# A four-layer image kernel: order of the first loads, the point at which C is spread, and values made beside keys

## The chip, the cores and the metric

One core of a Trainium2 chip. The metric is device time in microseconds (us) of one execution. Three runs of the kernel before gave 5076.55, 5076.93 and 5080.12 us; the median is 5076.93. The engines are named as in the profile: PE is TensorE (matmuls), PEld its weight loads, DVE is VectorE, ACT is ScalarE, POOL is GpSimd, and SP is SyncE, which here does nothing but issue DMAs.

## The reference

The input is x of shape (2, 128, 64, 64), float32: two images of 128 channels. Four layers follow each other. Cut to what matters here:

```python
# layer 0: 1x1 embed, two blocks of (layernorm, mamba, residual, layernorm, ffn, residual), 1x1 out, + x
u, z = split(norm(t) @ in_w.T);  u = silu(causal_conv4(u))
dt, Bm, Cm = split(u @ xproj_w.T, [8, 24])        # 8 + 16 + 16 columns
dt = softplus(dt @ dt_w.T + dt_b)
h = exp(dt * A) * h + (dt * u) * Bm               # 256 x 16 states, over 4096 positions
y = (sum_n(h * Cm) + u * D) * silu(z);  t = y @ out_w.T + t
# layer 1: attention over all 4096 positions with 3x3 convolutions
q, k, v = conv3x3(x, Wq), conv3x3(x, Wk), conv3x3(x, Wv)
x = x + conv1x1(softmax(q.T @ k / sqrt(128)) @ v.T, Wo)
# layer 2: the same shape of attention with dense (1x1) q, k, v
# layer 3: 3x3 convolutions at four scales, attention over the four, layernorm, 1x1 fusion
```

## The kernel before

The program's order on every engine is the order in which it was written (a manual schedule); tiles come from pools with a fixed number of buffers, and an instruction that takes a used buffer waits for the last reader.

**Start.** SP issues, in this order: constants `kc`, vectors `vec`, the eight chunks of image 0 (L93, 512 positions each), the embedding weights `we` (L125), and for each of the two mamba blocks `wl`, `cw` (taps, spread over the partitions, and the input projection) and `wd`; then three `raw` (the 3x3 weights of layer 1's q, k, v) and the chunks of image 1. For each block VectorE makes the folded taps `wu` (L152), and TensorE and VectorE spread the decay rates `an` to `am` (L155 to L162). `fold(which)` (L177 to L188, ten VectorE operations and two stores) turns one `raw` into the 18 filter slices of a reduced 3-tap convolution and stores them in DRAM as `ufold`.

**Layer 0.** There are 32 items (image, block, chunk of 512 positions), and each has 32 slots. In `slot(i, todo, t_)` one slot does one scan (L388, 128 lanes x 512 positions) of item i; four scans make a group, eight groups an item. A group's decay comes from `decay` (L377, ACT), its input from `times_b` (h = bb * pdu, L370), its result is multiplied with `cb` on POOL (L391) and summed on TensorE (`py`, L403). `spread_dt` (L359) copies a strip of dt to a tile `dtb` with four DMAs, `spread_dtu` (L364) does the like for dt*u on TensorE into `pdu`. Everything else is in `background(i)`, a list of what goes beside the scans in each slot, for items i-2 to i+2: input projection `pu`, `xproj` (`pd`, L321), `spread_bc` (L328 to L335), softplus, the norm (`pc`, `var`, `rs`, `pr`, `cen`, `xn`), gating, and the feed-forward (`ph`, `hid`, `pf`). Items -2 and -1 have no scans; in them the first items are prepared. `spread_bc` of item n is called once, in slot 14 of the item before:

```python
dr = dp.tile([2 * DS, CH], F32, name="dr", tag="dr")
nc.sync.dma_start(dr, st[i]["dbl"][R:])
for k in range(2):
    o = st[i]["bc", k] = sp.tile([P, 4, CH], F32, name=("bb", "cb")[k], ...)
    for q in range(4):
        nc.sync.dma_start(o[32 * q : 32 * q + 32]..., src.to_broadcast([32, 4 * CH]))
```

Both `bb` (B) and `cb` (C) go through DRAM (`dr`) and come back spread over 32 partitions.

**From layer 0 to layer 1.** While the last items end, `beginning()` is run step by step, as many steps in each slot as the string `beside` says. It loads q's and k's filters from `ufold` to the ring `uw`, and makes the queries of the first chunk and all keys of image 0. One conv over a chunk of 16 rows (1024 positions) is `inputs` (12 VectorE operations on `xt`, L599 to L610), `products_by` (18 matmuls `pa`, `pb`, L622) and `outputs` (2 ACT and 9 VectorE operations, L639 to L648). There are four chunks.

**Layers 1 and 2.** Four runs: (layer 1, image 0), (layer 1, image 1), (layer 2, image 0), (layer 2, image 1). A run has 128 units. In each unit TensorE makes 128 x 1024 scores (`pq`, L725), VectorE takes them out with the row maximum (L730), ACT takes exponentials every fourth unit (L740), `turn` (L755) transposes 128 x 2048 of them with one VectorE instruction in 32 x 32 blocks, and POOL, ACT's queue and SP's queue (L762 to L766) move the blocks to `pt`. LAG = 14 units later `product` (L775) multiplies `pt` with the turned values `vt`. The values of a layer-1 run are made in unit 13 by `values(r)`: per chunk `inputs` again, products with v's filters, `outputs` to `vs`, and `turned(cc)` (8 transposes `pvt` on TensorE and 2 copies on ACT). The two halves of v's filters are loaded in unit 1, and the first chunk's `inputs` are made in units 6 to 11.

Of the kernel before, what the change touches and what calls it, by code (L numbers as in the profile page):

```python
# [14 lines left out]
N = H * W  # L15
P = 128
# [51 lines left out]
def tile_conv_seq(ctx: ExitStack, tc, x, consts, vecs, wemb, wlay, wconv, wdt, wqkv, wsmall, wms, out):  # L68
# [23 lines left out]
    for c in range(NCH):  # L92
        nc.sync.dma_start(xv(0, c), x[0, :, c * RPC : (c + 1) * RPC, :])  # L93
# [20 lines left out]
    with tc.manual_schedule(), ExitStack() as s:  # L114
# [25 lines left out]
        wl, wu, wd, am = [], [], [], []  # L140
        for l in range(NL):
            w = wp.tile([P, NWL - DI], F32, name=f"wl{l}")
            nc.sync.dma_start(w, wlay[l][:, DI:])
            cw = sp.tile([P, KC + 1, DI], F32, name="cw", tag="h", bufs=5)
            nc.sync.dma_start(cw[:, :KC, :].rearrange("p k d -> p (k d)"), wconv[l : l + 1, :].to_broadcast([P, KC * DI]))
            nc.sync.dma_start(cw[:, KC, :], wlay[l][:, :DI])
            d = wp.tile([R, DI], F32, name=f"wd{l}")
            nc.sync.dma_start(d, wdt[l])

            u = wp.tile([P, KC, DI], F32, name=f"wu{l}")  # L150
            for k in range(KC):
                nc.vector.tensor_tensor(u[:, k, :], cw[:, KC, :], cw[:, k, :], ALU.mult)  # L152
            an = wp.tile([P, NJ * DS], F32, name=f"an{l}")
            nc.scalar.activation(an, vec[:, VEC[f"A_log{l}"] : VEC[f"A_log{l}"] + NJ * DS], AF.Exp)
            nc.vector.tensor_scalar(an, an, -1.0, None, ALU.mult)  # L155
            a = wp.tile([P, NJ, 4, 4], F32, name=f"am{l}")
            for g in range(4):
                pa = mm.tile([P, NJ, DS], F32, name="pa", tag="mm")
                nc.tensor.matmul(pa.rearrange("p j n -> p (j n)"), lhsT=four(g), rhs=an, start=True, stop=True)
# [3 lines left out]
            wl.append(w), wu.append(u), wd.append(d), am.append(a)  # L163
        raws = []
        for which in range(3):
            raw = sp.tile([P, 3, 3, C], F32, name="raw", tag="h", bufs=5)
            nc.sync.dma_start(raw.rearrange("p y x c -> p (y x) c"), wqkv[:, which])
            raws.append(raw)
        for c in range(NCH):
            nc.sync.dma_start(xv(1, c), x[1, :, c * RPC : (c + 1) * RPC, :])  # L170

        def fold(which):

# [150 lines left out]
            st[i]["dbl"] = sp.tile([NX, CH], F32, name="dbl", tag="dbl")  # L324
            nc.scalar.copy(st[i]["dbl"], st[i].pop("pd"))

        def spread_bc(i):

            dr = dp.tile([2 * DS, CH], F32, name="dr", tag="dr")
            nc.sync.dma_start(dr, st[i]["dbl"][R:])  # L330
            for k in range(2):
                o = st[i]["bc", k] = sp.tile([P, 4, CH], F32, name=("bb", "cb")[k], tag=("bb", "cb")[k], bufs=2)
                for q in range(4):
                    src = dr[k * DS + 4 * q : k * DS + 4 * q + 4, :].rearrange("(o m) f -> o (m f)", o=1)
                    nc.sync.dma_start(o[32 * q : 32 * q + 32].rearrange("p m f -> p (m f)"), src.to_broadcast([32, 4 * CH]))  # L335

        def dtproj(i, j):
            st[i]["pt", j] = mmt("pt")
# [131 lines left out]
        def background(i):  # L470

            todo = [[] for _ in range(NSL)]

            def at(t, f, *a):
                todo[t].append((f, a))

            n, p, q, r = i + 1, i - 1, i - 2, i + 2
            if has(q):
                at(3, gelu, q)
                at(6, ffn_down, q, (0, 1)), at(7, ffn_down, q, (2, 3)), at(9, ffn_add, q)  # L480
                at(11, out_mm, q), at(12, out_add, q)
            if has(p):
                at(7, y_out, p, 1), at(7, gate, p)
                at(9, mix_out, p), at(11, mix_add, p)
            if has(n):
                at(0, pu_taps, n, 0, (0, 1)), at(1, pu_taps, n, 0, (2, 3)), at(2, pu_out, n, 0)
                at(3, pu_taps, n, 1, (0, 1)), at(4, pu_taps, n, 1, (2, 3)), at(5, pu_out, n, 1)
                at(13, xproj, n), at(14, xproj_out, n), at(14, spread_bc, n)
                at(15, dtproj, n, 0), at(16, dtproj, n, 1), at(17, soft_plus, n), at(18, dt_end, n)
            if has(i):  # L490
                at(1, pz_mm, i, 0), at(3, pz_out, i, 0)
                at(5, pz_mm, i, 1), at(6, pz_out, i, 1)
            if has(i) or has(n):
                at(11, silu, i, n)
            if i == -1:
                for k in range(3):
                    at(8 * k + 2, fold, k)
            pair = [(k, second) for k, second in ((p, True), (r, False)) if has(k)]
            if has(r):
                at(10, embed, r), at(11, embed_out, r)  # L500
            w, m = {}, len(pair)
            for k, (it, second) in enumerate(pair):
                at(12 + 2 * k, ln_centre, w, k, it)
                at(13 + 2 * k, ln_square, w, k, it)
                at(27, ln_spread, w, k, m), at(28, ln_scale, w, k, it)
# [15 lines left out]
        def slot(i, todo, t_):  # L521
            t = i * NSL + t_
            g, m = divmod(t, 4)
            if m == 0 and 0 <= g + 3 < NG:
                spread_dt(g + 3)
            if m == 0 and 0 <= g + 1 < NG:
                spread_dtu(g + 1)
            if m == 0 and g % 2 == 1 and 0 <= g - 3 < NG:
                y_pair(g - 3)
# [1 line left out]
                scan(t)  # L531
            if 0 <= t + 4 < NT:
                decay(t + 4)
            if m == 3 and 0 <= g + 1 < NG:
                times_b(g + 1)
            for f, a in todo[t_]:
                f(*a)
# [72 lines left out]
                lambda: stt(d[5], x1(1), 4.0, d[5], ALU.mult, ALU.add),  # L610
            ]

        def products_by(which):

            pa = pss.tile([P, 4, QG], F32, name="pa", tag="s")
            pb = psq.tile([P, 2, QG], F32, name="pb", tag="q")
            for slot, dst in enumerate((pa[:, 2, :], pa[:, 0, :], pa[:, 3, :], pa[:, 1, :], pb[:, 0, :], pb[:, 1, :])):
                d = dlo[:, slot] if slot < 4 else sta["dhi"][:, slot - 4]
                for y in range(3):
                    rhs = d[:, y : y + 16, :].rearrange("p h j -> p (h j)")  # L620
                    lhsT = uw[:, where[which, slot // 3], 3 * (slot % 3) + y, :]
                    nc.tensor.matmul(dst, lhsT=lhsT, rhs=rhs, start=(y == 0), stop=(y == 2))  # L622
                yield
            return pa, pb
# [50 lines left out]
        def keys(r):  # L675
            k = sta["k"] = spa.tile([P, N], F32, name="k", tag="k")
            chunks(r, 1, lambda cc: k[:, cc * 4 * QG : (cc + 1) * 4 * QG])

        def values(r):
            vt = sta["vt"] = sp.tile([P, N // P, C], F32, name="vt", tag="vt")  # L680
            vs = {}

            def turned(cc):
                for i in range(2):
                    pt = psa.tile([P, 4, P], F32, name="pvt", tag="acc")
                    for a in range(4):
                        at = (4 * i + a) * P
                        nc.tensor.transpose(pt[:, a, :], vs[cc][:, at : at + P], ident)
                    at = (2 * cc + i) * 4
                    nc.scalar.copy(vt[:, at : at + 4, :], pt)  # L690

            def to(cc):
                if cc > 1:
# [124 lines left out]

        NALL = len(runs) * NU
        LO, HI = 0, 1  # L820
        def beginning():

            for which, half in ((0, LO), (0, HI), (1, LO)):
                load(which, half)
            for f in inputs(0, 0):
                f()
            yield
# [3 lines left out]
            outputs(*pp, [sta["q", 0, i] for i in range(4)], bias(0, 0))  # L831
            load(1, HI)
            k = sta["k"] = spa.tile([P, N], F32, name="k", tag="k")
            for cc in range(NCC):
# [12 lines left out]
        for k in range(8, 2 * NSL):  # L847
            if k == NSL:
                todo = background(NI + 1)
# [2 lines left out]
            slot(NI + k // NSL, todo, k % NSL)  # L852
        for _ in steps:
            pass
        layers.close()
        sp = s.enter_context(tc.tile_pool(name="ats", bufs=1, reuse_waits="tile"))
        psa = s.enter_context(tc.tile_pool(name="atpa", bufs=2, reuse_waits="tile", space=PSUM))
        psm = s.enter_context(tc.tile_pool(name="atpm", bufs=1, reuse_waits="tile", space=PSUM))
        for now in range(NALL + LAG + 10):
            r, u = divmod(now, NU)  # L860
            w = now % 8
            if now < NALL:
# [510 lines left out]
```

## Time and profile before

| what | value |
|---|---|
| median of 3 runs | 5076.93 us |
| profiled execution, its own time | 5077.7 us |
| its span, first to last instruction | 5075.9 us |
| mean granted TensorE clock | 0.948 |
| first scan starts / last scan ends | 84.94 / 2102.9 us |
| first `pq` of layer 1 | 2186.42 us |
| TensorE busy 2271 to 4400 | 2082.90 of 2129 us |
| layer 3 | about 4400 to the end |
| `cb<-dr`, `uw<-ufold`, `dtb<-dt`, from issue to landing | 7.6, 3.7, 2.0 us |

A timeline line gives the start, the duration, engine, line, operation, tiles and the number of instructions merged in it; the bracket has the engine's idle time before it and what released it. Lines of SP are the issuing of DMAs, not the transfers. In the page's section 2 each digit is the busy share of one of 40 slices (127 us each) in tenths.

### The profile page before, as it was taken

The page shows a single profiled execution, that of the slowest core. Times are in us where ns is not written, and L with a number is a line of the kernel's source. Part 1 is how long each engine was busy: PE and PEld are TensorE (multiplying, and loading weights), DVE is VectorE, ACT ScalarE, POOL GpSimd, SP SyncE. Part 2 cuts the span into 40 slices and gives each one's busy share as a digit, 9 for nine tenths or more (in the row PEclk, how much of TensorE's full clock was granted, in tenths as well). Part 3 has the DMA queues.
Part 4 walks back from the last instruction along what each step waited for, and adds up shares of the span by engine and source line. Part 5 has one row for each costly group of instructions (what it writes and reads, how often), then busy time and mean ns, then how long its engine had stood idle before and what let it go on. Part 6 is the DMA issues. An engine that isn't in the chain of part 4 may idle for free.

```text
span 5075.9 us, 48999 instructions
## 1 busy us (share of the span) xinstructions
PE 4683.8 (92%) x14797; PEld 2250.9 (44%) x14797; DVE 4097.5 (81%) x4416; ACT 2366.9 (47%) x3221; POOL 2316.3 (46%) x1948
## 2 busy tenths in 40 slices
PE   5889999999988899889999999999999999999997
PEld 1222222222222222356666666666666666333332
DVE  5999999999999999788888878667766775667775
ACT  4677777777777777522222222333333332323332
POOL 2777776766777777413332233233333332322331
PEclk8898889988999989899999999999999999999998
DMA  5333333333333333124443344444444443000000
GB/s 149 72 69 68 70 71 70 72 69 68 69 70 68 72 72 71 46 54 102 105 102 84 77 104 103 118 97 111 111 100 99 112 111 77 5 5 7 7 7 7
DMA packets 237016, 373.86 MB, mean 74 GB/s; under 512 B 88000, under 2 KB 88400, under 8 KB 228432
## 3 DMA queue, kind: packets, MB, share of 16 engines
q1 hardware_dynamic: 187600, 303.55, 25.8%
q10 hardware_dynamic: 49152, 67.17, 5.8%
q8 instruction: 118, 1.93, 0.2%
q14 instruction: 146, 1.20, 0.1%
HBM read 92.18 MB, written 9.83 MB: 20 GB/s over the span
## 4 chain that ended last, share of the span: by engine, by line
PE 47%; POOL 21%; DVE 13%; issue 11%; DMA 3%; ACT 3%; SPq 2%; ACTq 0%; DVEq 0%; POOLq 0%
POOL h L391 16%; PE po L775 13%; PE pq L725 13%; DVE tr L755 3%; DMA pt<-tr 2%; PE pf L1060 2%; SPq L766 2%; PE py L403 2%; PE pqkv L1087 2%; PE pu L292 1%; PE pw L1146 1%; POOL dtu L351 1%; PE pfus L1211 1%; POOL z L414 1%; PE psc L1111 1%
## 5 line engine op out<-in xcount | busy, mean ns | idle before, releaser
L762 POOL COPY pt<-tr 32x512 f32<-32x512 f32 x1024 | 656.1, 641 | 1468.2 <-DVE tr L755 738.8
L388 DVE TENSOR_TENSOR_SCAN h<-da,carry,h 128x512 f32<-128x512 f32 x1024 | 1241.4, 1266 | 60.4 <-ACT da L377 31.6
L391 POOL TENSOR_TENSOR h<-h,cb 128x2048 f32<-128x2048 f32 x256 | 1161.1, 4536 | 20.8 <-POOL carry L390 0.2
L725 PE MATMUL pq<-k,q 128*128 128x512 f32 x2048 | 965.1, 594 | 11.2 <-DVE sc L730 8.8
L775 PE MATMUL po<-pt,vt 128*128 128x256 f32 x4096 | 967.5, 380 | 2.4 <-DMA pt<-tr 2.4
L740 ACT ACTIVATE sc<-sc,nm 128x2048 f32<-128x2048 f32 x256 | 510.6, 1995 | 937.2 <-DVE nm L736 641.7
L730 DVE TENSOR_SCALAR_CACHE_REDUCE sc<-pq 128x1024 f32<-128x1024 f32 x512 | 624.9, 1222 | 359.8 <-PE pq L725 337.9
L775 PEld LDWEIGHTS po<-pt,vt 128*128 128x128 f32 x4096 | 780.5, 191 | 293.9 <-issue 211.1
L377 ACT ACTIVATE da<-dtb,am 128x512 f32<-128x512 f32 x1024 | 681.7, 684 | 222.1 <-DVE h L388 210.6
L755 DVE STREAM_TRANSPOSE tr<-sc 128x2048 f32<-128x2048 f32 x256 | 591.6, 2311 | 65.8 <-DMA pt<-tr 60.5
L370 DVE TENSOR_TENSOR h<-bb,pdu 128x2048 f32<-128x2048 f32 x256 | 581.7, 2272 | 77.4 <-PE py L403 29.3
L403 PE MATMUL py<-h,sel 128*32 128x512 f32 x2048 | 511.5, 643 | 1.6 <-POOL h L391 1.6
L725 PEld LDWEIGHTS pq<-k,q 128*128 128x128 f32 x2048 | 384.5, 191 | 289.5 <-issue 247.1
L364 PE MATMUL pdu<-dtu,fsel 128*128 128x512 f32 x512 | 326.5, 724 | 101.9 <-DVE h L370 101.8
L403 PEld LDWEIGHTS py<-h,sel 128*32 128x32 f32 x2048 | 115.7, 118 | 415.9 <-issue 408.9
L292 PE MATMUL pu<-xn,wu 128*128 128x512 f32 x512 | 246.2, 615 | 3.0 <-ACT xn L282 2.1
L364 PEld LDWEIGHTS pdu<-dtu,fsel 128*128 128x128 f32 x512 | 96.2, 215 | 308.3 <-DVE h L370 187.6
L390 POOL COPY carry<-h 128x4 f32<-128x4 f32 x256 | 47.5, 185 | 388.1 <-DVE h L388 383.5
L1153 DVE TENSOR_TENSOR ov<-v,pw 128x2048 f32<-128x2048 f32 x64 | 146.2, 2285 | 68.5 <-PE pw L1146 68.5
L1087 PE MATMUL pqkv<-f,ws 128*128 128x512 f32 x384 | 189.7, 619 | 3.0 <-DVE prod L1104 2.3
L1157 POOL TENSOR_TENSOR ov<-ov 128x2048 f32<-128x2048 f32 x16 | 72.6, 4537 | 257.6 <-DVE ov L1153 257.6
L351 POOL TENSOR_TENSOR dtu<-dt,u 128x1024 f32<-128x1024 f32 x32 | 75.0, 2345 | 189.7 <-ACT dt L345 189.7
(241 smaller groups left out, 5344.1 us busy)
## 6 DMA issues: line engine op xcount, KB each, us to landing
pt<-tr SPq DMA_DIRECT2D x2048, 64.0 KB, 2.0
dtb<-dt SPq DMA_DIRECT2D x1024, 64.0 KB, 2.0
pt<-tr ACTq DMA_DIRECT2D x1024, 64.0 KB, 2.2
bb<-dr SPq DMA_DIRECT2D x128, 256.0 KB, 4.6
cb<-dr SPq DMA_DIRECT2D x128, 256.0 KB, 7.6
uw<-ufold SPq DMA_DIRECT2D x14, 576.0 KB, 3.7
xt<-in_x SPq DMA_DIRECT2D x16, 256.0 KB, 5.0
xr<-in_x SPq DMA_DIRECT2D x16, 256.0 KB, 2.9
```

The costliest lines, as they stand in the source:

```text
L364: nc.tensor.matmul(pdu, lhsT=four(s_ % 4), rhs=st[i]["dtu"][:, s_ // 4, :], start=True, stop=True)
L370: nc.vector.tensor_tensor(h, st[i]["bc", 0], pdu.unsqueeze(1).to_broadcast([P, 4, CH]), ALU.mult)
L377: nc.scalar.activation(da, st[i]["dtb", s_], AF.Exp, scale=am[items[i][1]][:, j, gg, m : m + 1])
L388: nc.vector.tensor_tensor_scan(h[:, m, :], da, h[:, m, :], carries[b, l][:, j, gg, m : m + 1], ALU.mult, ALU.add)
L391: nc.gpsimd.tensor_tensor(h, h, st[i]["bc", 1], ALU.mult)
L403: nc.tensor.matmul(py[r : r + 32, :], lhsT=sel, rhs=st[i]["h", s_ + k][:, m, :], start=(m == 0), stop=(m == 3), tile_position=(0, r),)
L725: nc.tensor.matmul(pq[:, i, :], lhsT=sta["q", r, grp][:, it * P : (it + 1) * P], rhs=sta["k"][:, at : at + CH], start=True, stop=True)
L730: nc.vector.tensor_scalar(dst, pq, 1.0, None, ALU.mult, ALU.max, accum_out=sta["mx"][:, c2 : c2 + 1])
L740: nc.scalar.activation(sc, sc, AF.Exp, bias=nm, scale=scale, accum_out=sm[:, hh : hh + 1])
L755: nc.vector.transpose(tr, sta.pop(("sc", r, blk, hh)).rearrange("p (t r f) -> p r t f", r=NB, f=32))
L762: nc.gpsimd.tensor_copy(dst, src)
L775: nc.tensor.matmul(sta["po", r, grp], lhsT=sta["vt"][:, jt, :], rhs=rhs, start=(jt == 0), stop=(jt == N // P - 1))
```

## The change

It does three things.

1. The start is ordered anew. SP issues `kc`, `vec`, `we`, x chunk 0, then block 0's weights and x chunks 1 to 7, then block 1's weights. The taps and decay rates of block 0 are made at once (`prepare(0)`, the rates first), those of block 1 at slot 7 of item -1; the `raw` weights and image 1 are loaded at slot 1 of item -1, and the three folds come at slots 8, 9 and 10 of it (before: 2, 10 and 18). The first `spread_dtu` and `times_b` come at slots 19 and 26 of item -1.
2. `spread_bc` is in two calls: `bb` at slot 14, `cb` at slot 22.
3. Image 0's values are made in `beginning()`: after each keys product, a values product from the same `inputs`, with v's filters in a tile `uv` of their own, loaded once. They are turned in units 0 to 3 of the first run. For that run the load of v's filters in unit 1, the `inputs` in units 6 to 11 and `values` in unit 13 are gone; for image 1 they stay.

```diff
+        load_x(0, 0)
+        def load_layer(l):
+            cw = sp.tile([P, KC + 1, DI], F32, name="cw", tag="h", bufs=5)
+            nc.sync.dma_start(cw[:, KC, :], wlay[l][:, :DI])
+            nc.sync.dma_start(cw[:, :KC, :].rearrange("p k d -> p (k d)"), wconv[l : l + 1, :].to_broadcast([P, KC * DI]))
...
+        def prepare(l):
             an = wp.tile([P, NJ * DS], F32, name=f"an{l}")
...
+            u, cw = wp.tile([P, KC, DI], F32, name=f"wu{l}"), cws[l]
+            for k in range(KC):
+                nc.vector.tensor_tensor(u[:, k, :], cw[:, KC, :], cw[:, k, :], ALU.mult)
...
+        def load_rest():
+            for which in range(3):
+                raw = sp.tile([P, 3, 3, C], F32, name="raw", tag="h", bufs=5)
+                nc.sync.dma_start(raw.rearrange("p y x c -> p (y x) c"), wqkv[:, which])
...
+            for c in range(NCH):
+                load_x(1, c)
+        load_layer(0)
+        load_x(0, 1)
+        prepare(0)
+        for c in range(2, NCH):
+            load_x(0, c)
+        load_layer(1)
...
-        def spread_bc(i):
+        def spread_bc(i, k):
+            if k == 0:
+                st[i]["dr"] = dp.tile([2 * DS, CH], F32, name="dr", tag="dr")
+                nc.sync.dma_start(st[i]["dr"], st[i]["dbl"][R:])
...
-                at(13, xproj, n), at(14, xproj_out, n), at(14, spread_bc, n)
+                at(13, xproj, n), at(14, xproj_out, n), at(14, spread_bc, n, 0), at(22, spread_bc, n, 1)
...
             if i == -1:
+                at(1, load_rest), at(7, prepare, 1)
                 for k in range(3):
-                    at(8 * k + 2, fold, k)
+                    at(8 + k, fold, k)
+                at(19, spread_dtu, 0), at(26, times_b, 0)
...
-            if m == 0 and 0 <= g + 1 < NG:
+            if m == 0 and 1 <= g + 1 < NG:
                 spread_dtu(g + 1)
...
-            if m == 3 and 0 <= g + 1 < NG:
+            if m == 3 and 1 <= g + 1 < NG:
                 times_b(g + 1)
...
+            nc.sync.dma_start(uv, ufold[2])
...
             for cc in range(NCC):
                 pp = yield from products_by(1)
+                at = cc * 4 * QG
+                outputs(*pp, [k[:, at + i * QG : at + (i + 1) * QG] for i in range(4)], bias(0, 1))
+                if cc % 2 == 0:
+                    both = spa.tile([P, 2, 4 * QG], F32, name="vs", tag="tr", bufs=2)
+                vs[cc] = both[:, cc % 2, :]
+                pp = yield from products_by(2, uv)
                 ahead = inputs(0, cc + 1) if cc + 1 < NCC else []
                 for f in ahead[:8]:
                     f()
-                at = cc * 4 * QG
-                outputs(*pp, [k[:, at + i * QG : at + (i + 1) * QG] for i in range(4)], bias(0, 1))
+                outputs(*pp, [vs[cc][:, i * QG : (i + 1) * QG] for i in range(4)], bias(0, 2))
                 for f in ahead[8:]:
                     f()
-        beside = '2111001000112111111011010000'
+        beside = '21110010001121111110110111111111111111'
...
-                elif u == 1:
+                elif u == 1 and r:
                     load(2, LO), load(2, HI)
                     first = inputs(r, 0)
-                elif 6 <= u < 12:
+                elif 6 <= u < 12 and r:
...
-            if now < NALL and u == LAG - 1:
+            if now < NCC:
+                turned(now)
+            if r and now < NALL and u == LAG - 1:
                 values(r)
```

More of the change, by code (lines that the diff above doesn't have):

```diff
@@ L90, in tile_conv_seq, with load_x @@
         nc.gpsimd.memset(xt[:, b, 1 : H + 1, W + 1 : W + 2], 0.0)
-    for c in range(NCH):
-        nc.sync.dma_start(xv(0, c), x[0, :, c * RPC : (c + 1) * RPC, :])
+    def load_x(b, c):
+        nc.sync.dma_start(xv(b, c), x[b, :, c * RPC : (c + 1) * RPC, :])
     ud = ctx.enter_context(tc.tile_pool(name="ufold", bufs=1, space=bass.MemoryType.DRAM))
@@ L139, in tile_conv_seq @@
         nc.scalar.preload_act_table_set(EXP_LN_SET)
-        wl, wu, wd, am = [], [], [], []
-        for l in range(NL):
+        load_x(0, 0)
+        wl, wu, wd, am, cws = [], [], [], [], []
+        def load_layer(l):
+            cw = sp.tile([P, KC + 1, DI], F32, name="cw", tag="h", bufs=5)
+            nc.sync.dma_start(cw[:, KC, :], wlay[l][:, :DI])
+            nc.sync.dma_start(cw[:, :KC, :].rearrange("p k d -> p (k d)"), wconv[l : l + 1, :].to_broadcast([P, KC * DI]))
+            cws.append(cw)
             w = wp.tile([P, NWL - DI], F32, name=f"wl{l}")
             nc.sync.dma_start(w, wlay[l][:, DI:])
-            cw = sp.tile([P, KC + 1, DI], F32, name="cw", tag="h", bufs=5)
-            nc.sync.dma_start(cw[:, :KC, :].rearrange("p k d -> p (k d)"), wconv[l : l + 1, :].to_broadcast([P, KC * DI]))
-            nc.sync.dma_start(cw[:, KC, :], wlay[l][:, :DI])
             d = wp.tile([R, DI], F32, name=f"wd{l}")
             nc.sync.dma_start(d, wdt[l])
-            u = wp.tile([P, KC, DI], F32, name=f"wu{l}")
-            for k in range(KC):
-                nc.vector.tensor_tensor(u[:, k, :], cw[:, KC, :], cw[:, k, :], ALU.mult)
+            wl.append(w), wd.append(d)
+        def prepare(l):
             an = wp.tile([P, NJ * DS], F32, name=f"an{l}")
@@ L162, in tile_conv_seq @@
                     nc.vector.tensor_copy(a[at, :, g, :], pa[at, :, 4 * q : 4 * q + 4])
-            wl.append(w), wu.append(u), wd.append(d), am.append(a)
+            u, cw = wp.tile([P, KC, DI], F32, name=f"wu{l}"), cws[l]
+            for k in range(KC):
+                nc.vector.tensor_tensor(u[:, k, :], cw[:, KC, :], cw[:, k, :], ALU.mult)
+            wu.append(u), am.append(a)
         raws = []
[L165 to L170, printed above, removed]
+        def load_rest():
+            for which in range(3):
+                raw = sp.tile([P, 3, 3, C], F32, name="raw", tag="h", bufs=5)
+                nc.sync.dma_start(raw.rearrange("p y x c -> p (y x) c"), wqkv[:, which])
+                raws.append(raw)
+            for c in range(NCH):
[6 more added lines that the diff above has]
+        load_layer(1)
         def fold(which):
@@ L325, in xproj_out @@
             nc.scalar.copy(st[i]["dbl"], st[i].pop("pd"))
-        def spread_bc(i):
[L329 to L335, printed above, removed]
+        def spread_bc(i, k):
+            if k == 0:
+                st[i]["dr"] = dp.tile([2 * DS, CH], F32, name="dr", tag="dr")
+                nc.sync.dma_start(st[i]["dr"], st[i]["dbl"][R:])
+            dr = st[i]["dr"]
+            o = st[i]["bc", k] = sp.tile([P, 4, CH], F32, name=("bb", "cb")[k], tag=("bb", "cb")[k], bufs=2)
+            for q in range(4):
+                src = dr[k * DS + 4 * q : k * DS + 4 * q + 4, :].rearrange("(o m) f -> o (m f)", o=1)
+                nc.sync.dma_start(o[32 * q : 32 * q + 32].rearrange("p m f -> p (m f)"), src.to_broadcast([32, 4 * CH]))
         def dtproj(i, j):
@@ L611, in inputs, with products_by @@
             ]
-        def products_by(which):
+        def products_by(which, w=None):
             pa = pss.tile([P, 4, QG], F32, name="pa", tag="s")
@@ L620, in products_by @@
                     rhs = d[:, y : y + 16, :].rearrange("p h j -> p (h j)")
-                    lhsT = uw[:, where[which, slot // 3], 3 * (slot % 3) + y, :]
+                    lhsT = uw[:, where[which, slot // 3], 3 * (slot % 3) + y, :] if w is None else w[:, 3 * slot + y, :]
                     nc.tensor.matmul(dst, lhsT=lhsT, rhs=rhs, start=(y == 0), stop=(y == 2))
@@ L677, in keys, with turned @@
             chunks(r, 1, lambda cc: k[:, cc * 4 * QG : (cc + 1) * 4 * QG])
-        def values(r):
[L680 to L690, printed above, removed]
+        vs = {}
+        def turned(cc):
+            for i in range(2):
+                pt = psa.tile([P, 4, P], F32, name="pvt", tag="acc")
+                for a in range(4):
+                    at = (4 * i + a) * P
+                    nc.tensor.transpose(pt[:, a, :], vs[cc][:, at : at + P], ident)
+                at = (2 * cc + i) * 4
+                nc.scalar.copy(sta["vt"][:, at : at + 4, :], pt)
+        def values(r):
+            sta["vt"] = spa.tile([P, N // P, C], F32, name="vt", tag="vt")
             def to(cc):
@@ L820, in tile_conv_seq @@
         LO, HI = 0, 1
+        once = ExitStack()
+        uv = once.enter_context(tc.tile_pool(name="ato", bufs=1, reuse_waits="tile", side="right")).tile([P, 18, C], F32, name="uv")
         def beginning():
@@ L833, in beginning @@
             k = sta["k"] = spa.tile([P, N], F32, name="k", tag="k")
+            sta["vt"] = spa.tile([P, N // P, C], F32, name="vt", tag="vt")
             for cc in range(NCC):
                 pp = yield from products_by(1)
+                at = cc * 4 * QG
[4 more added lines that the diff above has]
+                pp = yield from products_by(2, uv)
                 ahead = inputs(0, cc + 1) if cc + 1 < NCC else []
@@ L854, in tile_conv_seq @@
             pass
+        once.close()
         layers.close()
```

## The prediction

> **What bounds the kernel now.** The page comes first:
>
> ```profile
> span 5075.9 us, 48999 instructions
> ...
> PE 4683.8 (92%) x14797; PEld 2250.9 (44%) x14797; DVE 4097.5 (81%) x4416; ACT 2366.9 (47%) x3221; POOL 2316.3 (46%) x1948
> ...
> PE   5889999999988899889999999999999999999997
> ...
> DVE  5999999999999999788888878667766775667775
> ```
>
> Two engines fill the span in turn: VectorE through the scans (about slices 2 to 16), TensorE through the attention. Both rows are thin in slice 1, and TensorE dips in slices 17 and 18, where scans give way to attention. The change works at those two seams, so the share of busy time over the whole is no guide; I read the timelines there. First TensorE in the start-up (start, duration, what; in brackets the idle time before it and its releaser):
>
> ```profile
> 21.16 1.06 PE L159 MATMUL pa<-an,fsel 128*128 128x32 f32 x4 [21.16 <-DVE an L155]
> ...
> 29.31 2.05 PE L217 MATMUL pe<-xt,we 128*128 128x512 f32 x2
> ...
> 46.74 9.90 PE L292 MATMUL pu<-xn,wu 128*128 128x512 f32 x16 [1.69 <-ACT xn L282]
> ...
> 63.02 3.38 PE L321 MATMUL pd<-u,wl 128*40 128x512 f32 x4
> ```
>
> and VectorE:
>
> ```profile
> 19.58 1.43 DVE L152 TENSOR_TENSOR wu<-cw 128x256 f32<-128x256 f32 x4 [15.18 <-DMA cw<-in_wlay]
> ...
> 84.94 4.81 DVE L388 TENSOR_TENSOR_SCAN h<-da,carry,h 128x512 f32<-128x512 f32 x4 [1.20 <-ACT da L377]
> ```
>
> Nothing real happens for 29.3 us: the folded taps wait for a weight load issued behind eight pieces of x, and the first matmul on x, `pe`, stands behind both layers' preparation in TensorE's program. SP's queue then shows how the spreads stand:
>
> ```profile
> 67.04 0.32 SPq L330 DMA_DIRECT2D dr<-dbl  x1
> 68.65 1.71 SPq L335 DMA_DIRECT2D bb<-dr  x4
> 70.41 1.81 SPq L335 DMA_DIRECT2D cb<-dr  x4
> 72.31 0.37 SPq L188 DMA_DIRECT2D ufold<-ulo  x1
> 73.30 0.34 SPq L188 DMA_DIRECT2D ufold<-uhi  x1
> 74.45 10.97 SPq L359 DMA_DIRECT2D dtb<-dt  x11
> ```
>
> At the other seam, TensorE's timeline:
>
> ```profile
> 2183.72 2.86 PE L622 MATMUL pb<-dhi,uw 128*128 128x256 f32 x12 [2.31 <-DVE dhi L608]
> 2186.42 1.02 PE L725 MATMUL pq<-k,q 128*128 128x512 f32 x2
> ...
> 2221.19 1.23 PE L786 MATMUL pr<-dg,kc 128*128 128x128 f32 x4 [5.07 <-DVE dg L780]
> 2222.21 5.81 PE L725 MATMUL pq<-k,q 128*128 128x512 f32 x8
> 2227.98 5.45 PE L622 MATMUL pa<-uw 128*128 128x256 f32 x24
> ...
> 2271.08 1.88 PE L725 MATMUL pq<-k,q 128*128 128x512 f32 x4
> ```
>
> Units 0 to 13 run from 2186.42 with gaps, then `values(0)` stands alone from 2227.98, and unit 14 begins at 2271.08. From there TensorE has hardly a gap, so every microsecond by which unit 14 starts earlier is kept.
>
> **Part by part.** The sum is made against the profiled execution, 5077.7 us (1.8 us outside its span, 0.8 above the median).
>
> *Start-up.* x chunk 0 and layer 0's weights go ahead of the rest, layer 1's preparation moves to slot 7 of item -1. `pe` then waits for chunk 0 and `prepare(0)`: on VectorE `sel` and `fsel` end at 4.4 (from 3.49, 0.37 and 0.62), `an` takes 0.17, four `pa` with their copies 2.9 us, and chunk 0, issued fourth at about 2.1, lands about 7 by the page's 5.0 for `xt`; so I put `pe` at 7.6 instead of 29.31. From there the chain is the same, 17.4 us to `pu`: 25.1, two `pu` of 9.9 to 35.0, `u` at 35.8. Layer 1's `an`, `am` (2.89) and `wu` (1.43) follow on VectorE to 41.3, and the three folds, 5.09 us each by their rows (45.76 to 61.02), end at 56.6. In before they lay beside `pu`; now their last part has no cover, because SP issues in order and the two stores of fold 2 (slot 10) stand ahead of `dr` (slot 14). `dbl`, ready at about 45, so waits: `dr` issues at 57 and not 46. This is what is late next. `dr` lands in 2.4, `bb` is issued 59.4 to 61.2 and takes 3.8 to land: 65.0. `h` (2.29, now ahead of `cen` 0.75) gives 68.0, with `dtb` issued in four steps of 1.0 us behind `bb`, landed about 66. First scan 68.0 against 84.94: **-17**. If `dr` landed with the stores untouched (1.6) and folds overlapped better, -20; if chunk 0, its weights or the raws land late, -11.
>
> A rule bears on `dr`. Row: `dr` alone issued 67.04, `bb` behind it 68.65, 1.6 us. The Trainium skill, "DMA: Bandwidth & Descriptors", Queues, rings and completion order, says that a completion signal on a DMA engine lands only after all earlier writes of that engine. `dr` would then also sit out the two ufold stores, 2.8 us by their own median in the trace of start-up: about 4.4, some 2 us more than I take. No row has `dr` behind a store; I lean to the row and keep the other in the range.
>
> *`cb` at slot 22.* SP's order per item becomes `dr`, four `bb`, eight `dtb`, four `cb`. No transfer is added. In the steady scans no compute engine waits for a DMA; its largest waits on VectorE are
>
> ```profile
> DVE h L388 <- ACT da L377: 23.3, 35, 1.1
> DVE h L370 <- PE py L403: 22.5, 22, 1.4
> ```
>
> in 1600 us. `cb` is used by POOL at slot 35, 13 slots of 2 us after its issue, 26 us; it lands in 7.6 by the page, and SP's longest wait on ACT in that stretch was 10.0. Slack 8 us or more: 0, between -2 (`bb` and `dtb` get the engines) and +2. Should the slack go, POOL's `h*C` (4.5 us) and `py` behind it are late, then VectorE for a buffer of `h`.
>
> *Image 0's values.* Removed: 48 VectorE `inputs` operations of a second pass, two loads of ufold in unit 1. Added: one 1.18 MB load of `uv`. TensorE's and ACT's counts stay. SP: `uv` takes memory that `hid` held until `pf` ends (2115), and `xr` for `out_mm` stands behind it, landing about 2121.4; `out_mm` takes it at 2124.84. `uv` is needed at 2138. Both hidden, by 3.4 and 17 us; if `xr` came later, the item's FFN tail moves by the excess. The first weights too stand behind the last `h*C` (to 2107.75), issued 4.5 us later than at 2103.19, landing 2112 to 2114, needed 2116.12.
>
> Through key chunk 0 nothing moves (TensorE at 2138.06). A chunk is a keys product and a values product, 7.77 each (2130.29 to 2138.06), 15.5 for TensorE; VectorE's part is 4.3 + 2.6 + 2 x 3.9 = 14.7. So TensorE sets the pace where keys alone were VectorE's (10.8 per chunk). I lay it out: values 0 from 2138.06, keys 1 to 2160 with `ph` between and 1.7 idle, values 1 with `pf` to 2172.4, `out_mm` to 2174.1, then four products: 2205.2. Part of this fills holes of before, the 4.00 us at `hid` among them. Scores start 18.8 later than 2186.42; first eviction on VectorE +18.4 (2207.5).
>
> Units 0 to 13 now hold no `inputs` (8.3 us on VectorE) and four groups of 8 `pvt` (1.04 each, in TensorE's gaps). VectorE there: 2189.13 to 2232.03 was 42.9, now 36.6 minus the small idles that a turn's DMAs leave: eviction 12 ends at 2240, unit 14 at 2240.1 instead of 2271.08, -31. SP may add: a turn's eight DMAs took 5.0 us to issue and 2.0 to land, and turns come each 5.0 to 5.6. I take **-29**; -22 if the turns wait on it or `ph` comes late, -32 if nothing does.
>
> Here the clock gate counts. Row: after the 5.07 us gap, `pr` took 1.23 and eight `pq` 5.81, where without such a gap they take 0.61 (at 2291.74) and 3.46 (from 2279.69, two by two); 3.0 us lost; after 2.91 and 2.71 nothing. The Trainium skill, "TensorE: Matmul & The Clock Gate", Part 1, has half rate after an idle window of about 3.4 us and full rate after 3.4 busy. By the rule a crossing costs some 1.7, by the row 3.0. My longest gap in units 4 to 13 is 2.6, so 0 by both; 3.0 per crossing stays in the range, and the one of before (3.0) is in the -29.
>
> Sum: -17 + 0 - 29 = -46: 5077.7 - 46 = 5031.7, on the medians 5031.
>
> **The rivals.**
> 1. Smaller (20%): `dr` behind the fold stores by the rule, the raws late, and turns paced by SP: -11 + 0 - 22 = -33, so 5044. For it: every DMA of both seams goes through SP. Against: the loads ended by 35 us in before, turns waited only 0.24 us for their transfers.
> 2. Larger (11%): the folds do not hold `dr`, TensorE's idle time in the seam (28.9 us from 2111 to 2271, and 10 of slow clock) is nearly all recovered: -20 - 33 = -53, so 5024. For it: the holes at `hid` and `dg` belong to it. Against: SP is in order.
> 3. Slower (4%): `cb` lands late in each item, POOL is held at the first `h*C`. Over 32 items it must cost 46/32 = 1.4 us each to eat the gain, and (46 + 10)/32 = 1.8 for a slowdown of 10 us; that is `cb` landing 8.4 + 1.8 = 10 us or more later than I put it. At 3 us an item it gives 5031 + 96 = 5127. For it: `cb` is the slowest transfer of the page (7.6), now behind eight `dtb` whose issue waits for ACT. Against: 26 us of distance.
> 4. No effect (3%): the seams are filled but something behind them (POOL, the turns) ends at the same time, 5067 to 5087. Against: scans are bound by VectorE and the attention by TensorE, and both start earlier.
>
> **The numbers.** Forecast 62%: 5026 to 5038. Range 5020 to 5050, which takes in rival 2's 5024, rival 1, and unknowns of the parts. About 0.2% (10 us) is what a measurement of this kernel can tell from no change: faster 0.93, same 0.03, slower 0.04.
>
> **What would show it.** `pe` near 7.6; first scan near 68, `dr` issued right after fold 2's last store; last scan about 17 earlier than 2102.9; SP's wait of POOL on `cb` absent; `inputs` 48 fewer; the pair keys and values at 15.5 per chunk; first score 19 later after the last scan than in before, unit 14 at 137 after it instead of 168 (2271.08 - 2102.9). A first scan after 74, a wait POOL `h` <- DMA `cb`, or a TensorE gap over 3 us in units 4 to 13 would show my steps wrong.

## The result, and the profile after

The changed kernel took 5035.91 us (median of 4 runs, 5034.91 to 5036.79) beside 5078.52 us for the kernel before on the same chip: a ratio of 0.9916, with a 95% interval of 0.99 to 0.9932, or 42.6 us less. The forecast was 5031 with a range of 5020 to 5050. One execution, the profiled one of run a_start, took 7030 us at a granted clock of 0.628; it is left out of every median, and of its trace one wait alone is used.

The page of the changed kernel:

```profile
span 5033.7 us, 48953 instructions
...
PE 4670.3 (93%) x14797; PEld 2243.1 (45%) x14797; DVE 4073.5 (81%) x4368; ACT 2367.4 (47%) x3221; POOL 2314.4 (46%) x1948
...
PE   6889999999988899899999999999999999999997
```

The shares hardly moved. TensorE lost 13.5 us of busy time with the same 14797 matmuls, VectorE has 48 operations less. TensorE's row shows one tenth more in slice 1 and one in slice 18, and little else; the gain has to be read in the timelines.

**The start.** TensorE's timeline (start, duration, what, idle time before it and its releaser):

```profile
4.77 1.06 PE L161 MATMUL pa<-an,fsel 128*128 128x32 f32 x4 [4.77 <-DVE an L157]
...
7.71 2.05 PE L233 MATMUL pe<-xt,we 128*128 128x512 f32 x2
...
25.14 9.78 PE L308 MATMUL pu<-xn,wu 128*128 128x512 f32 x16 [1.69 <-ACT xn L298]
...
43.53 3.64 PE L337 MATMUL pd<-u,wl 128*40 128x512 f32 x4
```

Up to here every step is where it was put: `pe` at 7.71 (forecast 7.6), `pu` at 25.14 (25.1). Then SP's queue, and VectorE:

```profile
51.02 0.32 SPq L204 DMA_DIRECT2D ufold<-uhi  x1
58.60 0.32 SPq L204 DMA_DIRECT2D ufold<-ulo  x1
60.12 0.32 SPq L204 DMA_DIRECT2D ufold<-uhi  x1
60.53 0.40 SPq L347 DMA_DIRECT2D dr<-dbl  x1
63.19 1.71 SPq L352 DMA_DIRECT2D bb<-dr  x4
65.00 2.50 SPq L376 DMA_DIRECT2D dtb<-dt  x4
67.55 2.67 SPq L352 DMA_DIRECT2D cb<-dr  x4
```

```profile
69.97 2.29 DVE L387 TENSOR_TENSOR h<-bb,pdu 128x2048 f32<-128x2048 f32 x1 [9.88 <-DMA bb<-dr]
72.17 0.74 DVE L285 SCALAR_TENSOR_TENSOR cen<-cen,vec,pr 128x512 f32<-128x512 f32 x1
72.83 4.80 DVE L405 TENSOR_TENSOR_SCAN h<-da,carry,h 128x512 f32<-128x512 f32 x4
```

`dbl` was ready at 47.8 (forecast about 45), but `dr` was issued at 60.53, straight behind the last store of fold 2, and VectorE then stood idle for 9.88 us until `bb` came. The first scan started at 72.83: 12.1 us earlier than in before, not 17. (Run c_values, which has the start of before, had its first scan at 82.56; against that trace it would be 9.7.)

**The scans.** From the first scan's start to the last scan's end it is 2018.0 us in before (84.94 to 2102.9) and 2018.5 in after (72.83 to 2091.35). In the changed kernel's list of waits between 85 and 2090 us no compute engine waits for a DMA. The page's DMA rows (tile, queue, count, size, median time to landing) are

```profile
bb<-dr SPq DMA_DIRECT2D x128, 256.0 KB, 4.4
cb<-dr SPq DMA_DIRECT2D x128, 256.0 KB, 4.7
```

so `cb`, which took 7.6, now lands in 4.7 and nobody gains by it.

**From layer 0 to layer 1.** The last scans in VectorE's timeline of the changed kernel end at 2091.35:

```profile
2087.72 3.63 DVE L405 TENSOR_TENSOR_SCAN h<-da,carry,h 128x512 f32<-128x512 f32 x3
```

TensorE's timeline:

```profile
2162.35 5.34 PE L641 MATMUL pa<-uw 128*128 128x256 f32 x24
2167.53 2.75 PE L641 MATMUL pb<-dhi,uw 128*128 128x256 f32 x12
2170.12 5.34 PE L641 MATMUL pa<-uw,uv 128*128 128x256 f32 x24
2175.30 2.75 PE L641 MATMUL pb<-dhi,uv 128*128 128x256 f32 x12
2177.89 5.34 PE L641 MATMUL pa<-uw 128*128 128x256 f32 x24
...
2193.43 1.88 PE L746 MATMUL pq<-k,q 128*128 128x512 f32 x4
...
2223.48 1.04 PE L807 MATMUL pr<-dg,kc 128*128 128x128 f32 x4 [1.82 <-DVE dg L801]
2224.36 3.60 PE L746 MATMUL pq<-k,q 128*128 128x512 f32 x8
2229.47 1.98 PE L746 MATMUL pq<-k,q 128*128 128x512 f32 x4 [1.51 <-DVE sc L751]
```

A chunk of keys and values is 15.54 us (2162.35 to 2177.89), back to back; the first score is 102.1 us behind the last scan (83.5 in before), and unit 14 begins at 2229.47, 138.1 us behind it (168.2 in before). The stretch between the last scan and unit 14 in the view of busy time by stretch (length; busy us of PE, PEld, DVE, ACT, POOL with instructions; granted clock; DMA share and GB/s), of before and then of after:

```profile
2103.00:2271.00 168.00, 137.90 (x485) 87.58 (x485) 125.61 (x226) 44.82 (x64) 25.63 (x25) 0.96 0.21 59
```

```profile
2091.35:2229.50 138.15, 128.45 (x487) 85.80 (x485) 93.36 (x174) 44.75 (x64) 18.91 (x20) 1.00 0.16 47
```

TensorE does the same matmuls in both (two records more in the second). Its idle time falls from 30.1 to 9.7 us, which is 20.4, and its busy time by 9.5, at a granted clock of 1.00 where it was 0.96. Together that is the 30. Some 6.5 of the 9.5 can be placed: 3.0 is the crossing that the prediction shows, and two more of before are

```profile
2157.15 5.40 PE L448 MATMUL pf<-hid,wl 128*128 128x512 f32 x8 [4.00 <-ACT hid L440]
2243.18 4.54 PE L622 MATMUL pb<-dhi,uw 128*128 128x256 f32 x12 [1.98 <-DVE dhi L608]
```

where eight `pf` take 3.70 and twelve `pb` 2.75 in other places of the same trace; the granted clock was 0.68 in the first and 0.61 in the second. The other 3.0 was not taken apart.

Between these two traces, then: -12.1 at the start, +0.6 in the scans, -30.1 at the second seam, -0.6 after it: -42.2 of span.

### The profile page after: what moved, and what is told of

Same layout as the page of the kernel before. It is cut to its first block, busy times and chain, and to the rows that moved or that the text cites. A ratio compares the mean times of both kernels' runs of the same rounds, so it can differ in the third digit from the quotient of the medians.

```text
span 5033.7 us, 48953 instructions
## 1 busy us (share of the span) xinstructions
PE 4670.3 (93%) x14797; PEld 2243.1 (45%) x14797; DVE 4073.5 (81%) x4368; ACT 2367.4 (47%) x3221; POOL 2314.4 (46%) x1948
## 3 DMA queue, kind: packets, MB, share of 16 engines
q8 instruction: 118, 1.93, 0.2%
## 4 chain that ended last, share of the span: by engine, by line
PE 40%; POOL 23%; DVE 14%; issue 12%; DMA 5%; SPq 4%; ACT 3%; ACTq 0%; DVEq 0%; POOLq 0%
POOL h L408 19%; PE pq L746 10%; PE po L796 10%; DVE tr L776 5%; DMA pt<-tr 4%; SPq L787 4%; PE pf L1094 2%; PE pqkv L1121 2%; PE pa L641 2%; PE pw L1180 1%; POOL dtu L368 1%; POOL z L431 1%; PE py L420 1%; PE pfus L1245 1%; PE psc L1145 1%
```

## The experiments

Each is named by its label; ratios are to the kernel before, run beside it on the same chip.

**a_start: the new order of the start alone.** `cb` stays beside `bb` in slot 14, the values stay in unit 13.

```diff
-                    at(8 * k + 2, fold, k)
+                    at(8 + k, fold, k)
+                at(1, load_rest), at(7, prepare, 1), at(19, spread_dtu, 0), at(26, times_b, 0)
```

> Only the new order of the start; bb and cb still go out together in slot 14 and the values stay in unit 13. Theory (the parts add, each at its own seam): first scan at 73 to 76 us (it was 84.94 before and 72.83 with the whole change; here the four cb stand ahead of the first dtb, 1.8 to 2.7 us on SP), last scan to unit 14 unchanged at 168 us, time 9 to 12 us under the kernel before. Rival (the start-up gain is later lost while SP or the first items catch up, and only the values move the end): first scan early all the same, but the last scan within 3 us of 2102.9 and the time within 4 us of before.

5067.29 us (17 executions) against 5076.19, 8.9 us less; the ratio is 0.9984 (0.9977 to 0.9991, that is 4.6 to 11.7 us). This is at the lower edge of what was expected of the theory, and more than the 4 us that the rival allowed; where the last scan ends in this run is not known. In VectorE's timeline of its trace the first scan waits 3.67 us for `da`, with the four `cb` issued ahead of the first `dtb`; f_cb14 below has the same wait.

**b_cb22: `cb` at slot 22 alone.**

```diff
-                at(14, spread_bc, n)
+                at(14, spread_bc, n, 0), at(22, spread_bc, n, 1)
```

> Only cb in slot 22 in place of slot 14. Theory: cb is always early enough, nothing on an engine waits for these transfers; time within 3 us of before, first scan 1 to 3 us earlier at most because the first dtb no longer stand behind cb. Rival (cb and dtb hinder each other in every item): cb lands in under 5 us where it took 7.6, and the time falls by over 10 us; the other rival, cb late for POOL, would raise the time by 1.5 us or more an item, 48 us or more.

5073.8 us, ratio 0.9996 (0.9988 to 1.0005), which includes no change. `cb` lands in 4.7 us here too, yet first to last scan is 2018.1 us (81.31 to 2099.41). Neither rival holds: a shorter transfer is no gain where nobody waited for the longer one, and `cb` is not late. Only the wait of 1.20 us for `da` ahead of the first scan of before is gone here.

**c_values: image 0's values beside the keys, alone.** The part of the diff from `uv` on.

> Only the values of image 0 beside the keys; start and cb as before. Theory: last scan at 2102.9 as before, unit 14 at 138 us after it where it was 168.2, time 29 to 31 us under before. Rival (part of the later seam's gain needs the new start or cb's later place, since SP's queue at the end of the scans is freer with them): 20 to 26 us.

5048.64 us, ratio 0.9947 (0.993 to 0.9963): 27.5 us less. The trace has the last scan's end at 2099.56, and unit 14 begins with

```profile
2237.67 1.98 PE L727 MATMUL pq<-k,q 128*128 128x512 f32 x4 [1.51 <-DVE sc L732]
```

138.1 us later, exactly as with the whole change. The seam gains its 30 without help of the other parts; the median is 1.5 us short of the 29 to 31 expected, within the interval. The three medians add to 8.9 + 2.4 + 27.5 = 38.8 against 42.6 and 40.0 in two measurements of the whole; of the three the 2.4 cannot be told from no change.

**d_fold2_late: the third fold behind the spreads in SP's order.**

```diff
-                    at(8 + k, fold, k)
+                    at((8, 9, 21)[k], fold, k)
```

> The whole change, with the third fold at slot 21 of item -1 in place of slot 10, so that its two stores stand on SP behind dr, the four bb and the first dtb, not ahead of them. Theory (fold 2's stores hold dr on SP): dr issues at about 48 where it was 60.53, first scan at 61 to 63 where it was 72.83, time 9 to 12 us under the changed kernel. Rival (VectorE itself or the landing of bb and dtb sets the first scan, not the order on SP): first scan not before 69, time within 4 us of the changed kernel.

5025.82 us, ratio 0.99 (0.9885 to 0.9915), where the whole change had 0.9916 and, in h_after, 0.9922. SP's queue:

```profile
49.73 0.32 SPq L204 DMA_DIRECT2D ufold<-ulo  x1
51.24 0.32 SPq L204 DMA_DIRECT2D ufold<-uhi  x1
51.66 0.41 SPq L347 DMA_DIRECT2D dr<-dbl  x1
54.27 1.71 SPq L352 DMA_DIRECT2D bb<-dr  x4
```

`dr` is out 8.9 us earlier and the first scan starts at 63.87, 9.0 earlier. The expectation missed one thing: `dr` went at 51.66 and not 48, because fold 1's stores still stood ahead, and the first scan was 0.9 later than the 61 to 63 given. The third fold still runs on VectorE ahead of `h` (51.13 to 60.32), as slowly as in the changed kernel; only its stores moved. So the order on SP is what held the start back, and the rival is out.

**h_after, f_cb14: the whole change again, and with `cb` back in slot 14.**

```diff
-                at(14, spread_bc, n, 0), at(22, spread_bc, n, 1)
+                at(14, spread_bc, n, 0), at(14, spread_bc, n, 1)
```

> The changed kernel itself, to stand on the same chip as the three beside it. 40 to 45 us under the kernel before; first scan within 2.5 us of 72.83.

> The whole change with cb back in slot 14 beside bb. Theory (cb's place pays once, in the start, since the first dtb no longer stand behind it; in the steady scans it is free): first scan 4 to 6 us later than in the changed kernel, with ACT waiting for dtb, and the time 4 to 6 us above it. Rival (cb's place pays nothing): first scan and time within 2 us of the changed kernel.

The whole change: 5036.27 us against 5076.26, ratio 0.9922 (0.991 to 0.9934), first scan at 71.86. With `cb` back: 5039.14, ratio 0.9929 (0.9915 to 0.9942), 2.9 us more. The two intervals of the ratios overlap, but the five times of each, taken on one chip, do not (5035.16 to 5037.37 and 5038.38 to 5041.34), and the traces show where it lies. With `cb` in slot 14 VectorE's timeline has

```profile
68.04 2.29 DVE L387 TENSOR_TENSOR h<-bb,pdu 128x2048 f32<-128x2048 f32 x1 [10.04 <-DMA bb<-dr]
70.25 0.74 DVE L285 SCALAR_TENSOR_TENSOR cen<-cen,vec,pr 128x512 f32<-128x512 f32 x1
74.66 4.81 DVE L405 TENSOR_TENSOR_SCAN h<-da,carry,h 128x512 f32<-128x512 f32 x4 [3.67 <-ACT da L394]
```

Here the first scan waits 3.67 us for `da`, whose `dtb` went out behind four `cb`. With `cb` in slot 22 that wait is absent. `bb` came 1.0 us earlier in this execution, so the first scan is only 2.8 later; without that it would be 3.8, still a little short of the 4 to 6 expected. First to last scan: 2017.7 with slot 14 (74.66 to 2092.37), 2018.2 with slot 22 (71.86 to 2090.03). So `cb`'s place pays once, in the start, and nothing per item. It also accounts for most of what lies between a_start's 8.9 us and the 12.1 by which the whole change brought the first scan forward, as far as starts that vary by a microsecond or two can show.

**e_inputs_twice: the shared inputs made a second time.**

```diff
+                for f in inputs(0, cc):
+                    f()
                 pp = yield from products_by(2, uv)
```

> The whole change, but the 12 VectorE operations of inputs are made again for the values product of each chunk, 48 operations more. Theory (the later seam gains because one set of inputs serves two products, which leaves TensorE the bound of the stretch at 15.5 us a chunk): a chunk of keys and values then takes about 2 x 10.8 us as the two separate passes did, first score 20 to 27 us later, time 18 to 27 us above the changed kernel. Rival (the gain is that the values fill idle time at the tail of layer 0 and in its holes, the inputs themselves being hidden): under 8 us above it.

5063.17 us, ratio 0.9975 (0.9965 to 0.9985): 26.9 us above the whole change on the same chip, at the upper end of what the theory said. TensorE's timeline:

```profile
2188.02 6.80 PE L641 MATMUL pa<-uw,uv 128*128 128x256 f32 x24 [4.42 <-DVE uw L620]
2194.66 2.75 PE L641 MATMUL pb<-dhi,uv 128*128 128x256 f32 x12
2197.25 5.34 PE L641 MATMUL pa<-uw 128*128 128x256 f32 x24
...
2210.01 7.74 PE L641 MATMUL pa<-uw,uv 128*128 128x256 f32 x24 [4.42 <-DVE uw L620]
...
2220.18 1.88 PE L746 MATMUL pq<-k,q 128*128 128x512 f32 x4
```

A chunk now takes 21.6 us (key products from 2175.68 to 2197.25), twice the 10.8 of a pass by itself. TensorE waits 4.42 us ahead of each values product (4.37 ahead of the first), and the 24 `pa` products behind such a gap take 6.80 and 7.74 us instead of 5.34. Nearly the whole gain of the seam goes when the inputs are no longer shared: filling holes at the tail of layer 0 is not what pays.

**g_folds_early: block 1's taps, the raw weights and the folds ahead of everything that `dr` needs.**

```diff
-            if i == -1:
-                at(1, load_rest), at(7, prepare, 1)
+            if i == -2:
+                at(22, prepare, 1)
+            if i == -1:
+                at(1, load_second)
                 for k in range(3):
-                    at(8 + k, fold, k)
+                    at(1 + k, fold, k)
```

(`load_layer(1)` without its wide weights and `load_rest` with the raw weights alone stand ahead of x chunks 2 to 7; `load_second` loads image 1.)

> The whole change, with block 1's taps and the three raw weights loaded ahead of x chunks 2 to 7, prepare(1) at slot 22 of item -2 and the folds at slots 1 to 3 of item -1, so that their stores are issued long before dr is ready and no fold runs beside dt*u on POOL. Theory (the folds and their stores cost the start-up about 12 us through SP's order): folds without the 1.6 to 2.5 us operations, dr issued at 47 to 48 and bb behind it after 1.6 us and not 2.6, first scan at 60 to 62 and the time 10 to 13 us under the changed kernel. Rival (another wait of nearly the same length takes its place: dtb's landing, pr, or a late raw): first scan at 66 or later, under 6 us gained.

5023.84 us against 5036.27 for the whole change beside it, ratio 0.9898 (0.9884 to 0.9911): 12.4 us less. `dr` was issued at 47.54 and the first scan started at 60.63. No fold operation takes over 0.56 us. One point of the expectation failed: `bb` followed `dr` after 2.66 us again, since the eight loads of image 1 had held up the fold stores and the last of them went out at 47.12, 0.4 us ahead of `dr`.

**i_image1_late, g_folds_again: the loads of image 1 behind the spreads.**

```diff
-                at(1, load_second)
+                at(30, load_second)
```

> The early folds, and the eight loads of image 1 at slot 30 of item -1 in place of slot 1, so that the fold stores go out as soon as they are made and all have landed when dr is issued. Theory (a store ahead on the queue costs dr about 1.0 us: 2.6 us from dr to bb behind one, 1.6 without): 1.6 us from dr to bb, no wait of VectorE for a store, h 1 to 2 us earlier; the first scan stays at 59.5 to 61 since pr and cen come last there, the time within 3 us of the early folds. Rival (dr's time has nothing to do with the stores and lies in the re-ordered start): 2.6 us again.

> The early folds once more, to stand beside it on the same chip: 51 to 54 us under the kernel before, 2.6 us from dr to bb.

5023.18 (ratio 0.9897, 0.9882 to 0.9911) and 5024.8 us (0.9898, 0.9882 to 0.9915), against 5076.4 for the kernel before: the two are level, and both are faster than the changed kernel. SP's queue and VectorE with image 1 late:

```profile
42.40 0.32 SPq L211 DMA_DIRECT2D ufold<-uhi  x1
48.07 0.32 SPq L354 DMA_DIRECT2D dr<-dbl  x1
49.70 1.71 SPq L359 DMA_DIRECT2D bb<-dr  x4
```

```profile
56.33 2.29 DVE L394 TENSOR_TENSOR h<-bb,pdu 128x2048 f32<-128x2048 f32 x1 [13.96 <-DMA bb<-dr]
60.48 0.75 DVE L292 SCALAR_TENSOR_TENSOR cen<-cen,vec,pr 128x512 f32<-128x512 f32 x1 [1.86 <-PE pr L288]
61.15 4.80 DVE L412 TENSOR_TENSOR_SCAN h<-da,carry,h 128x512 f32<-128x512 f32 x4
```

With the last store 5.7 us ahead, `bb` follows `dr` after 1.63 us; in the second run of the early folds it was 1.93 and not the 2.6 expected, since there `dr` was issued 1.1 us behind the store and not 0.4. `h` came 0.8 and 0.95 us earlier than in the two runs of the early folds, a little under the 1 to 2 given. The microsecond buys nothing here, because the norm of the next chunk (`pr`, then `cen`) now comes last ahead of the first scan, and `dr` can hardly go earlier: `dbl` itself was ready only at 48.05.

**k_dtu_vector: dt*u of item 0 on VectorE.** Measured in one execution.

```diff
-            nc.gpsimd.tensor_tensor(w["dtu"], w["dt"], w["u"], ALU.mult)
+            (nc.gpsimd if i else nc.vector).tensor_tensor(w["dtu"], w["dt"], w["u"], ALU.mult)
```

> The changed kernel with dt*u of item 0 alone on VectorE, behind the folds, in place of POOL. Theory (VectorE's fold operations are slow while POOL works on a product of two tensors): the first slow one, 2.46 us, falls to 0.56, those beside POOL's nt and rs stay at about 1.6; dr is issued some 1.9 us earlier in relation to the start of the folds. Rival (the folds are slowed by transfers in flight, not by POOL): all three stay slow.

POOL in the changed kernel, and then the three slow fold operations on VectorE there:

```profile
50.62 2.34 POOL L368 TENSOR_TENSOR dtu<-dt,u 128x1024 f32<-128x1024 f32 x1 [29.25 <-ACT dt L362]
54.72 1.35 POOL L272 TENSOR_TENSOR nt<-nt,ve 1x512 f32<-1x512 f32 x1 [1.76 <-ACT nt L267]
56.90 1.25 POOL L277 TENSOR_TENSOR rs<-rs,nt 1x512 f32<-1x512 f32 x1 [0.83 <-ACT nt L273]
```

```profile
50.91 2.46 DVE L193 TENSOR_TENSOR ulo<-raw 128x384 f32<-128x384 f32 x1
...
54.87 1.61 DVE L197 SCALAR_TENSOR_TENSOR uhi<-raw 128x384 f32<-128x384 f32 x1
...
56.92 1.66 DVE L199 SCALAR_TENSOR_TENSOR ulo<-raw,uhi 128x384 f32<-128x384 f32 x1
```

Each slow one starts at or inside a POOL product and ends 0.4 us behind it. With dt*u off POOL, the first is back at 0.55 us; the two beside `nt` and `rs` stay at 1.61 and 1.66, though they start 2.6 us earlier in the execution. `dr` comes 17.9 us behind the start of the folds (40.05 to 57.92) and not 19.8 (40.75 to 60.53). POOL's product is the cause of the first; that the other two moved along with `nt` and `rs` says the same of them. That execution took 5032.9 us.

## Why the prediction held, and where it missed

- **The second seam: right in mechanism and size.** 138.1 us from last scan to unit 14 against the 137 given; 15.54 per chunk against 15.5; first score 18.6 later against 18.8; 36.0 us from it to unit 14 against 34.9. e_inputs_twice shows why: with the inputs made again the 27 us are gone. The term for the clock was too small in words: some 6.5 of the 30 us are products at a low clock in before, in three places, and the sum named one of them (3.0). Since the layout was counted from products at the fast rate, it took in the others unnamed. One sum is wrong: 42.9 less the 8.3 of the inputs is 34.6, not 36.6. The stretch measured about 37 (2196.23 to 2233.4), since VectorE there waits for the first scores, 0.5 to 1.4 us each; that the written figure is so near is luck.
- **The clock gate.** The row and the skill's rule, as the prediction took them, both gave 0 for the changed kernel, and so it was: no gap over 2.03 us in units 4 to 13 and no slow product. But a gap has no one price. In e_inputs_twice those of 4.37 and 4.42 cost from 1.5 (6.80 against 5.34) to 2.8 us (6.86 for 18 `pa` that otherwise take 4.05), from just under the prediction's 1.7 for the rule to just under its 3.0 for the row. And in before a gap of 1.98 was followed by 1.8 us of loss where 2.91 and 2.71 cost nothing: the length of the last gap alone does not decide. The prediction did not look at that place, and no run here shows what does decide.
- **The start: right in its steps, too large by 4.9 us.** Three terms were mis-sized. Folds: put at 5.09 each, the third took 9.2 us (50.91 to its last store at 60.12), since POOL's products fell beside it; the folds of before had run with POOL idle, so the row did not hold for the new place. With the folds begun 0.6 earlier than forecast, `dr` went 3.5 us late. `dr`: 2.66 to `bb` instead of 2.4. `h` began, with `bb`, 5.1 us behind the last issue of `bb` (69.97 less 64.9) and not 3.8; why it took longer was not followed up. The first scan is then 68.0 + 3.5 + 0.3 + 1.3 = 73.1 against 72.83 measured.
- **`dr` behind a store.** The row (1.6) and the estimate by the skill's rule (about 4.4) bracketed the time from `dr` to `bb`: 2.6 with a store 0.4 us ahead, 1.93 with one 1.1 ahead, 1.6 with none near. The direction of the rule is shown; the full price is not paid. (The 2.8 in that estimate is the median of `uhi`'s stores alone; that of `ulo`'s was 6.0.)
- **`cb` at slot 22.** Zero in the scans, as given. That its place would help the start (3.67 us of waiting for `da` without it) was counted in the start-up chain without being named as the second part's. One reading was too broad: in the scans of before the profile does put one wait of a compute engine down to a DMA (POOL, 2.7 us, `dtb`).
- **Rivals.** The smaller one came near at the start (-12.1 against its -11), but largely by luck: the fold stores did stand ahead of `dr`, yet 3.5 of the 4.9 us are folds that POOL slowed, which it does not name. The raws were not late, and the turns hardly waited (0.24 us, as in before). The larger one fails at the start, where the folds did hold `dr`; its view of the seam was near, 30 against 33. The slower one is excluded: no wait for `cb` in any scan. No effect is excluded by the 42.6 us.

## What to carry to other kernels

A queue that issues in order is part of the critical path: a store that waits for late, unimportant work holds back every later transfer, and here moving the folds out of `dr`'s way was worth 12.4 us, more than the new start had gained by itself (8.9). A gain at a seam is found by laying out the slower engine's work from the rows and asking which engine sets the pace; sharing one operand preparation between two products moved the bound from VectorE to TensorE. A duration taken from a row holds only for the neighbours that it had there: look at what the other engines do in the new place.

## What was not expected of the hardware

- VectorE operations of 0.56 us took up to 2.46 us when they met a product of two tensors on POOL, and ended 0.4 us behind it, even where POOL's product had a single partition (1x512, 1.25 us). The same shows at the second seam (L619: 2.84 us where it otherwise takes 0.67, beside POOL's `z` from 2100.74 to 2103.46; before has it too, 2.85). The Trainium skill, "SBUF — State Buffer", section "SBUF: two separate sides", describes it: VectorE and POOL share a pair of ports that is locked for a whole instruction, and a VectorE operation with two inputs from SBUF, or one in a two-port mode, blocks against a POOL operation that reads SBUF. The three operations slowed here have two inputs. In h_after, the same kernel, POOL's first product met one with a single tensor input instead (L198: 2.49 us where it otherwise takes 0.36), so a single input is no protection; which mode it runs in the trace does not show. The prediction did not look at any of this when it moved the folds.
- The start of the same program varies from execution to execution by 1 to 2.4 us in the traces here: first scan at 84.94 and 82.56 in two kernels with the same start, 72.83 and 71.86 in the same kernel. First to last scan takes from 2016.7 to 2019.3 us in the twelve traces other than a_start's.
